# One step for an expert's 32 small list matmuls, and the last expert's row fetch moved ahead of expert 6's first way back, in a fused attention and mixture-of-experts kernel

## The chip, the cores and the metric

The kernel runs on one core of a Trainium2 chip. The metric is the device time in microseconds of one execution of the program; lower is better. Profile times count from the start of the profiled execution's span. The engines are named as the profile does: PE (matmuls), PEld (its weight loads, which overlap), DVE (vector), ACT (activations), POOL (GpSimd, which here also issues all indirect DMAs) and SP (issues the plain DMAs).

## The reference

Four blocks follow each other, each as x = x + layernorm(block(layernorm(x))) over 4096 tokens of width 256: a gated attention, a low-rank feed-forward, a 16-head attention with relu weights, and a mixture of 8 experts. Only the last is touched:

```
S = sigmoid(xt @ Wg).T                    # 8 x 4096 scores
G, I = top_k(S, 1024)                     # each expert picks its 1024 best tokens
ex = xt[I]
hid = gelu(einsum('ekh,ehf->ekf', ex, W1) + b1)
out = (einsum('ekf,efh->ekh', hid, W2) + b2) * G
new_x = zeros_like(xt).at[I].add(out)     # a token may be picked by several experts
```

## The kernel before, in words

The first three blocks end at about 981 us of the span; the experts take the rest. Their stage begins at line 1706. PE, DVE and ACT (and POOL from expert 6 on) run in the order in which the program is written there.

**Search and list.** For each expert a `Search` (line 1757) finds the score of its 1024th token by ten rounds of comparing and counting. A `List` (line 1837) then makes the token numbers: `sort` marks the chosen ones, `rank` counts them (two matmuls and a row of small DVE operations), `chunks` and four `places` build one-hot operands on DVE (line 1914, each 128 x 1024 in bf16), four `collect` multiply them on PE (line 1924, eight 16 x 128 matmuls each, in bf16), ACT copies the result (line 1933), and `gather` folds it with one matmul (line 1936), casts it to `idx` on DVE (line 1938) and issues eight indirect fetches of token rows on POOL (`got`, line 1948). The `places` write tiles `at` from a pool of three buffers, so the fourth can be written only when the first `collect` has read its tile.

**The agenda.** List and search steps are cut into pieces with an assumed DVE cost and the earliest group of tokens beside which they may run (lines 1829 and 1897). `go_on_with_lists(u, time, most)` (line 2300) is called after pieces of expert work; it takes at most one step off the agenda if the time left over from the last is under 0.3, the step is due, and its cost is at most `most`. So the list of expert e+1 is made while expert e runs.

**Expert work.** Experts 0 to 2 and 7 run plain (`feed_forward`, line 2218): 512 tokens a group `u`, two groups an expert. Experts 3 to 6 run both groups at once by seven block products (`feed_forward_by_seven`, line 2168): for each of four f, products a, b, c, d start, then a gets a second product (`a2` below), c a second (`c2`) and d a second (`d2`). Each product shows as two matmuls in the profile. DVE adds between them: u2 + b (line 2194), u2 + c (line 2196, before `c2` may overwrite c), + d (line 2198, before `d2`), and after them lines 2205 and 2208. There are two list calls in each f: one between `a2` and `c2`, with `most` 1.5 (line 2202), and one after `d2` (line 2210).

**The way back.** `project_back` (line 2250) makes four 128 x 256 products `py` for each group; DVE adds the bias and scales by the gate into `y` (lines 2274 and 2275, four buffers), and POOL issues an indirect DMA that adds the rows into `acc_d` in memory (line 2276). Scatters of one expert must wait for those before them, but for expert 6, where they are declared independent.

**The end.** During expert 7 the accumulated rows are read back by SP (`read_back`, line 1996, all six first ones behind every scatter), normalized by DVE statistics, POOL's powers and ACT's scaling (line 2013), and added to the output; expert 7's own rows are fetched by index: `xg`, the block's input rows (`fetch_last`, line 2317, eight fetches), and `accg`, the sums so far (line 2027). The plan `beside_last` (line 2077) says beside which product each of these is put. The final rows go out by indexed scatter (line 2052), behind all other stores. `fetch_last` is called between the two halves of expert 6's way back (line 2214), so its eight POOL fetches stand between that expert's fourth and fifth scatter.

Tile `xs[4]` (`ADDED` is 5) holds input rows of the block; its four stores to `out` are issued before the experts begin, and it is not used after that. `xs[0]` to `xs[3]` already serve as scratch for the seven-product sums (line 2130).

Of the kernel before, what the change touches and what calls it, by code (L numbers as in the profile page):

```python
# [12 lines left out]
BF16 = mybir.dt.bfloat16  # L13
# [6 lines left out]
P = 128  # L20
D = 256
DC = D // P
TB = 512
# [22 lines left out]
NE = 8  # L46
# [5 lines left out]
ADDED = 5  # L52
# [22 lines left out]
def kernel(  # L75
# [33 lines left out]
    B, S, _ = x_in.shape  # L109
# [18 lines left out]
    xs = []  # L128
# [93 lines left out]
    with ExitStack() as st1:  # L222
# [96 lines left out]
        for r in range(2):  # L319
            for j in range(4):  # L320
                at = 32 * j + HD * r
# [126 lines left out]
        wk = st1.enter_context(tc.tile_pool(name="l0", bufs=2))  # L448
# [66 lines left out]
        time = {"now": 0.0, "spent": 0.0}  # L515
# [85 lines left out]
        def open_block(t):  # L601

            d = {"t": t}
            r, stats, _, shift = stats_steps("a", lambda: xs[t])
            d["r"] = r

            def scales(part=slice(0, NJ)):

                if part.start == 0:
                    r["ve"] = small.tile([P, 2, NJ], F32, tag="vea2", name="vea2")  # L610
                    rs = r["both"] = small.tile([P, 2, NJ], F32, tag="rsa2", name="rsa2")
                    r["rs"], r["rs2"] = rs[:, 0, :], rs[:, 1, :]
                ve = r["ve"]
                nc.vector.tensor_scalar(ve[:, 0, part], r["mv"][:, part, 1], EPS, None, ALU.add)
                nc.vector.tensor_scalar(ve[:, 1, part], r["mv"][:, part, 1], 1.0 + EPS, EPS * EPS, ALU.mult, ALU.add)
                nc.gpsimd.tensor_tensor(r["both"][:, :, part], ve[:, :, part], mhalf2[:, :, part], ALU.pow)

            def apply(i0):
                if i0 == 0:
                    d["n"] = wk.tile([P, NJ, D], F32, tag="n", name="n")  # L620
                for i in (i0, i0 + 1):
                    nc.vector.tensor_scalar(
                        d["n"][:, i, :], xs[t][:, i, :], r["mv"][:, i, 0:1], r["rs2"][:, i : i + 1],
                        ALU.subtract, ALU.mult,
                    )

            if t == 0:

                early, late = (lambda part=part: scales(part) for part in halves_0)
                return d, [  # L630
                    *stats[:2], (0.0, early), *stats[2:], (0.0, late), (0.0, lambda: apply(0)), (0.0, lambda: apply(2)),
                    (0.0, shift),
                ]
            return d, [*stats, (0.0, scales), (POW, shift), (0.0, lambda: apply(0)), (0.0, lambda: apply(2))]
# [358 lines left out]
        d, steps = open_block(0)  # L993
# [18 lines left out]
        left, ffn, take = [], ([], [], []), {}  # L1012
        for t in range(NB):
# [51 lines left out]
            left = from_hidden  # L1065
            ffn = feed_forward(t, lambda d=d: d["y"], ahead)
            chains.insert(0, chains.pop())
            d = coming
# [33 lines left out]
    with ExitStack() as st3:  # L1102

        wts = st3.enter_context(tc.tile_pool(name="l1w", bufs=3))
        wk = st3.enter_context(tc.tile_pool(name="l1a", bufs=2))
# [541 lines left out]
        for b in range(B):  # L1647
            after = open_row(None if b else next_hs, last=b + 2 == B) if b + 1 < B else None
            for qh in range(BPB):
# [13 lines left out]
                for q2 in range(halves):  # L1663
                    for g in range(NG):
                        for kt in range(0, KT, halves):
# [5 lines left out]
                            step = kt // halves  # L1671
# [34 lines left out]
    with ExitStack() as st4:  # L1706
# [46 lines left out]
        wk = st4.enter_context(tc.tile_pool(name="moe", bufs=2))  # L1753
        ps = st4.enter_context(tc.tile_pool(name="moe_ps", bufs=2, space=PSUM))
        QT = NTILE // 4

        class Search:
# [71 lines left out]
            def steps(self, behind=0):  # L1829

                spent = 0.15 + 0.6 * len(self.es)
                return [
                    (spent, behind, lambda: self.compare(0)),
                    *((spent + 0.85, behind, lambda r=r: self.tick(r)) for r in range(NBITS // NPER)),
                ]

        class List:


# [57 lines left out]
            def steps(self):  # L1897

                behind = max(QPE * self.e - 3, 0)
                return [  # L1900
                    (0.5, behind, self.sort),
                    (2.6, behind, self.rank),
                    (1.2, behind, self.chunks),
                    (1.4, behind, lambda: (self.places(0), self.places(1))),
                    (1.4, behind, lambda: (self.places(2), self.collect(0), self.places(3), self.collect(1))),
                    (0.3, behind, lambda: (self.collect(2), self.collect(3))),

                    (0.3, behind + 1, self.gather),
                ]

            def places(self, part):
                js = slice(part * QT, (part + 1) * QT)
                self.at[part] = wk.tile([P, P, QT], BF16, tag="at", name="at", bufs=3)
                nc.vector.tensor_tensor(
                    self.at[part],
                    self.lo[:, js].unsqueeze(1).to_broadcast([P, P, QT]),
                    each[:, :, js],
                    ALU.is_equal,
                )
# [37 lines left out]
        lists = [List(e) for e in range(NE)]  # L1957
# [149 lines left out]
        QPE = NC // NJ  # L2107
# [18 lines left out]
        def by_seven(e):  # L2126

            return 3 <= e < NE - 1
# [39 lines left out]
        def feed_forward_by_seven(e):  # L2168

            w1, w2 = weights[e]  # L2170
            hid = [wk.tile([P, FC, TB], F32, tag="hid", name="hid") for _ in range(QPE)]
            (b11, b21), (t3, b22) = ([xT[QPE * e + q][:, c, :] for c in range(DC)] for q in range(QPE))
            t1, t2, t4 = (seven[name] for name in ("T1", "T2", "T4"))
            half = DFF // 2
            s3 = w1[:, 0, half:DFF]
            s1, s2, s4 = (seven[name] for name in ("S1", "S2", "S4"))

            def product(bank, a, b, start, stop, f):
                nc.tensor.matmul(bank, lhsT=a[:, f * P : (f + 1) * P], rhs=b, start=start, stop=stop, skip_group_check=not start)

            gelus = []

            def gelu(n, f, src):
                gelus.append(nc.scalar.activation(hid[n][:, f, :], src, AF.Gelu, bias=mb1[:, e * FC + f : e * FC + f + 1]))

            HC = FC // 2
            for f in range(HC):
                a, b, c, d = (ps.tile([P, TB], F32, tag="mm", name=f"ph{k}", bufs=5) for k in range(4))
                u2 = seven[f"sum{f % 2}"]
                c22, c21, c12 = hid[1][:, HC + f, :], hid[0][:, HC + f, :], hid[1][:, f, :]  # L2190
                product(a, w1[:, 0, 0:half], b11, True, True, f)
                nc.scalar.copy(u2, a)
                product(b, s2, t2, True, True, f)
                nc.vector.tensor_tensor(u2, u2, b, ALU.add)
                product(c, s3, t3, True, True, f)
                nc.vector.tensor_tensor(c22, u2, c, ALU.add)
                product(d, s1, t1, True, True, f)
                nc.vector.tensor_tensor(c22, c22, d, ALU.add)
                product(a, w1[:, 1, 0:half], b21, False, True, f)
                gelu(0, f, a)  # L2200
                if f < HC - 1:
                    go_on_with_lists(QPE * e, 3.2, 1.5)
                gelu(1, HC + f, c22)
                product(c, w1[:, 1, half:DFF], t4, False, True, f)
                nc.vector.tensor_tensor(c21, u2, c, ALU.add)
                gelu(0, HC + f, c21)
                product(d, s4, b22, False, True, f)
                nc.vector.tensor_tensor(c12, u2, d, ALU.add)
                gelu(1, f, c12)
                go_on_with_lists(QPE * e, 3.0)  # L2210
            for q in range(QPE):
                if q == 0 and by_seven(e + 1):
                    weight_sums(e + 1, gelus[-1])
                if q == 1 and e == NE - 2:
                    fetch_last()
                project_back(QPE * e + q, hid[q])

# [74 lines left out]
        searches = [Search(0), Search(1), Search(2, 3), Search(4, 5, 6, 7)]  # L2292
        agenda = []
# [3 lines left out]
                agenda.extend(lists[e].steps())  # L2297
        left = [0.0]

        def go_on_with_lists(u, time, most=4.0):  # L2300
            left[0] = max(left[0] - time, 0.0)
            if agenda and left[0] < 0.3 and agenda[0][1] <= u and agenda[0][0] <= most:
                spent, _, step = agenda.pop(0)
                left[0] += spent
                step()

        first = ps.tile([P, TB], F32, tag="mm", name="idle", bufs=5)
        for n, (_, _, step) in enumerate(searches[0].steps() + lists[0].steps()):
            step()
            if n == 1:  # L2310
                nc.vector.memset(parts[:, 0 : P + NC], 0.0)
            if step == lists[0].rank:
                keep_busy(first, 8)
# [3 lines left out]
        def fetch_last():  # L2317

            for c in range(NC):
                last.fetch(xg[:, c, :], x_d, c)  # L2320

        for u in range(NE * QPE):
            e, q = divmod(u, QPE)
# [44 lines left out]
```

## Time and profile before

| | |
|---|---|
| runs | 1497.52 us median of 3 (1497.13, 1497.52, 1506.65) |
| profiled execution | 1498.18 us, of which the span is 1496.4 us |
| mean granted PE clock | 0.985 |
| busy share of the span | PE 96%, PEld 52%, DVE 63%, ACT 48%, POOL 35% |
| experts, first product of expert 0 to last of expert 7 | 1012.8 to 1484.5 us |
| from PE's last matmul to the end | 11.9 us |
| one DVE `places` operation (line 1914) | 684 ns, 32 of them |
| one indirect fetch of `got` or `xg` on POOL (line 1948) | 1033 ns, and 0.30 us to the next |
| one adding scatter on POOL (line 2276) | 1580 ns, 56 of them |

A timeline row gives the start in us, the duration in us, engine, line, operation, the operands as out<-in with shapes, how many in succession (x16), and in brackets how long the engine had been idle and what ended that. A windows row gives a stretch of the span, its length, the busy time of each engine with the number of instructions, the mean granted PE clock, the DMA share and GB/s.

### The profile page before, as it was taken

How to read it: one execution, taken by the hardware profiler on the slowest of the kernel's cores; microseconds unless marked ns; L12 is line 12 of the kernel's file. 1: busy time of each engine (PE TensorE's matmuls, PEld its weight loads, DVE VectorE, ACT ScalarE, POOL GpSimd, SP SyncE). 2: the span in 40 equal slices, each digit the busy share in tenths (PEclk: the TensorE clock that was granted, in tenths of full speed). 3: DMA queues.
4: the chain of work that ended last, by engine and by line, in shares of the span. 5: the costliest groups of instructions: out<-in, count | busy, mean ns of one | idle time of the engine just before them, and what ended most of it. 6: DMA issues, size and time to landing. Idle time of an engine off the chain costs nothing. (4 is left out here: it accounts for less than half of the span.)

```text
span 1496.4 us, 24269 instructions
## 1 busy us (share of the span) xinstructions
PE 1443.0 (96%) x9240; PEld 780.3 (52%) x9240; DVE 936.5 (63%) x2221; ACT 713.7 (48%) x1182; POOL 518.3 (35%) x646
## 2 busy tenths in 40 slices
PE   8999999999899999999999999949999999999996
PEld 4666666666532333332333235517566656756764
DVE  5456655576456589659974987885545756355355
ACT  4244455444466766777676787722221232232142
POOL 4123231232250223422441323413435324553574
PEclk9999999999999999999999999979999999999998
DMA  8400000002334242533153211151424233343374
GB/s 215 139 1 1 1 1 1 1 0 82 116 99 130 69 135 64 160 99 106 61 183 114 98 52 37 44 162 37 103 29 118 46 87 59 75 100 57 64 189 114
DMA packets 91885, 121.58 MB, mean 81 GB/s; under 512 B 24925, under 2 KB 64250, under 8 KB 91642
## 3 DMA queue, kind: packets, MB, share of 16 engines
q1 hardware_dynamic: 70000, 73.09, 15.6%
q0 software_dynamic: 21712, 46.94, 13.8%
q8 instruction: 72, 1.18, 0.3%
q14 instruction: 43, 0.35, 0.1%
q10 hardware_dynamic: 58, 0.01, 0.0%
HBM read 66.90 MB, written 53.12 MB: 80 GB/s over the span
## 5 line engine op out<-in xcount | busy, mean ns | idle before, releaser
L1542 PE MATMUL po<-w,vaug 128*17 128x512 f32 (+1 forms) x2304 | 269.3, 550 | 2.8 <-DVE turned L1592 2.6
L2259 PE MATMUL py<-w,hid 128*128 128x256 f32 x1024 | 231.0, 383 | 2.1 <-ACT hid L2240 2.1
L2259 PEld LDWEIGHTS py<-w,hid 128*128 128x128 f32 x1024 | 193.3, 192 | 33.1 <-issue 4.7
L1530 DVE TENSOR_SCALAR w<-sc 128x1024 f32<-128x1024 f32 x152 | 184.8, 1221 | 35.2 <-PE sc L1514 32.8
L1522 ACT ACTIVATE w<-sc 128x512 f32<-128x512 f32 x256 | 152.9, 597 | 112.4 <-ACT w L1526 50.5
L1514 PE MATMUL sc<-q,kT 32*128 32x512 f32 (+1 forms) x2304 | 190.5, 412 | 2.2 <-ACT w L1522 1.0
L1514 PEld LDWEIGHTS sc<-q,kT 32*128 32x128 f32 x2304 | 86.2, 183 | 173.7 <-ACT w L1522 92.0
L2276 POOL DMA_INDIRECT acc_d<-y,idx x56 | 88.5, 1580 | 169.3 <-issue 37.4
L2240 ACT ACTIVATE hid<-ph,mb 128x512 f32<-128x512 f32 (+1 forms) x72 | 45.9, 638 | 160.3 <-PE ph L2233 134.5
L1526 ACT ACTIVATE w<-sc 128x512 f32<-128x512 f32 x203 | 120.2, 592 | 0.0
L2233 PE MATMUL ph<-xT,w 128*128 128x512 f32 (+1 forms) x288 | 115.3, 553 | 0.3 <-DVE xT L2124 0.3
L1528 ACT ACTIVATE w<-sc 128x1024 f32<-128x1024 f32 x104 | 106.7, 1026 | 0.0
L1948 POOL DMA_INDIRECT got<-tok_d,idx x64 | 66.1, 1033 | 75.4 <-DVE idx L1938 57.1
L1542 PEld LDWEIGHTS po<-w,vaug 128*17 128x17 f32 x2304 | 41.9, 96 | 95.3 <-issue 71.8
L2233 PEld LDWEIGHTS ph<-xT,w 128*128 128x128 f32 x288 | 52.5, 190 | 51.8 <-issue 47.7
L2274 DVE TENSOR_TENSOR y<-py,mb 128x256 f32<-128x256 f32 x56 | 23.6, 421 | 70.5 <-PE py L2259 55.8
L724 PE MATMUL pg<-nT,wh 128*128 128x512 f32 x128 | 61.6, 613 | 1.5 <-ACT nT L663 1.5
L850 PE MATMUL py<-wo,oT 128*128 128x256 f32 x256 | 61.9, 385 | 0.0
L740 PE MATMUL pv<-wh,nT 128*128 128x512 f32 x128 | 59.7, 593 | 0.0
L850 PEld LDWEIGHTS py<-wo,oT 128*128 128x128 f32 x256 | 47.3, 190 | 17.1 <-issue 9.6
L915 ACT ACTIVATE hid<-ph,vec 128x512 f32<-128x512 f32 x64 | 39.8, 685 | 27.3 <-PE ph L906 27.1
L588 POOL TENSOR_TENSOR x<-x,y 128x1024 f32<-128x1024 f32 x13 | 30.6, 2353 | 57.4 <-ACT y L577 57.4
(340 smaller groups left out, 2399.1 us busy)
## 6 DMA issues: line engine op xcount, KB each, us to landing
q<-q_d POOLq DMA_DIRECT2D x16, 1024.0 KB, 6.0
w<-in_L_ffn_W_dram SPq DMA_DIRECT2D x16, 1024.0 KB
q_d<-parts SPq DMA_DIRECT2D x48, 256.0 KB
kT<-k_d POOLq DMA_DIRECT2D x16, 512.0 KB, 4.1
k_d<-parts SPq DMA_DIRECT2D x24, 256.0 KB
acc_d<-logits SPq DMA_DIRECT2D x8, 512.0 KB
tok_d<-hg SPq DMA_DIRECT2D x30, 128.0 KB
x<-in_L_attn_x_dram SPq DMA_DIRECT2D x7, 512.0 KB
```

The costliest lines, as they stand in the source:

```text
L724: nc.tensor.matmul(pg, lhsT=wh[:, c, HID + e * P : HID + (e + 1) * P], rhs=d["nT"][:, c, :], start=(c == 0), stop=(c == DC - 1),)
L850: nc.tensor.matmul(py, lhsT=d["oT"][:, e, :], rhs=wo[:, e, :], start=(e == 0), stop=(e == EC - 1))
L1514: nc.tensor.matmul(sc[:, m * n : (m + 1) * n], lhsT=row["kT"][t][rows, r, (kt + m) * P : (kt + m + 1) * P], rhs=row["q"][qh, t][rows, r, p ...
L1522: nc.scalar.activation(w[:, 0, :], singles[0], AF.Relu)
L1526: nc.scalar.activation(w[:, 1, :], singles[1], AF.Relu)
L1528: nc.scalar.activation(w[:, 2:4, :], pair, AF.Relu)
L1530: nc.vector.tensor_scalar(w[:, 2:4, :], pair, 0.0, None, ALU.max)
L1542: nc.tensor.matmul(po[32 * j : 32 * j + HD + 1, weighed(halves, r)], lhsT=row["v"][:, kt + m, HQ * t + 4 * r + j, :], rhs=w[:, j, m * n : ...
L1948: return nc.gpsimd.indirect_dma_start(out=dst, out_offset=None, in_=rows[:, :], in_offset=self.at_chunk(c), bounds_check=NT - 1, oob_is_er ...
L2233: nc.tensor.matmul(ph, lhsT=w1[:, c, f * P : (f + 1) * P], rhs=xT[u][:, c, h * n : (h + 1) * n], start=(c == 0), stop=(c == DC - 1),)
L2259: nc.tensor.matmul(py, lhsT=hid[:, f, i * P : (i + 1) * P], rhs=w2[:, f, :], start=(f == 0), stop=(f == FC - 1),)
L2276: scatter = nc.gpsimd.indirect_dma_start(out=acc_d[:, :], out_offset=lists[e].at_chunk(k), in_=y, in_offset=None, bounds_check=NT - 1, oob ...
```

## The change

- A list's four `collect` run in one step, behind all four `places`; before, two of them ran in the step of the later `places`, and two in a step of their own. To make this possible, the third and fourth `places` write into the two halves of `xs[4]`, viewed as bf16, and the pool tile `at` has two buffers.
- The list call in the middle of an f of the seven-product form takes steps by their kind (costs 0.5, 1.2 and 1.4: `sort`, `chunks`, `places`), not by an upper bound on their cost. `collect` and `gather`, at 0.3, can no longer be taken there. The other calls have no bound.
- `fetch_last` is called before the first half of expert 6's way back.
- The first list, which is made ahead of the loop, keeps one `collect` behind each `places` by a function of its own.

```diff
+        def in_stored(half):
+            room = xs[ADDED - 1].rearrange("p j d -> p (j d)")[:, half * TB : (half + 1) * TB]
+            return room.bitcast(BF16).rearrange("p (a b) -> p a b", b=QT)
...
-                    (1.4, behind, lambda: (self.places(2), self.collect(0), self.places(3), self.collect(1))),
-                    (0.3, behind, lambda: (self.collect(2), self.collect(3))),
+                    (1.4, behind, lambda: (self.places(2), self.places(3))),
+                    (0.3, behind, lambda: [self.collect(part) for part in range(4)]),
...
-                self.at[part] = wk.tile([P, P, QT], BF16, tag="at", name="at", bufs=3)
+                if part < 2:
+                    self.at[part] = wk.tile([P, P, QT], BF16, tag="at", name="at", bufs=2)
+                else:
+                    self.at[part] = in_stored(part - 2)
...
-                    go_on_with_lists(QPE * e, 3.2, 1.5)
+                    go_on_with_lists(QPE * e, 3.2, True)
...
-                if q == 1 and e == NE - 2:
+                if q == 0 and e == NE - 2:
                     fetch_last()
                 project_back(QPE * e + q, hid[q])
...
-        def go_on_with_lists(u, time, most=4.0):
+        def go_on_with_lists(u, time, within=False):
             left[0] = max(left[0] - time, 0.0)
-            if agenda and left[0] < 0.3 and agenda[0][1] <= u and agenda[0][0] <= most:
+            if agenda and left[0] < 0.3 and agenda[0][1] <= u and not (within and agenda[0][0] not in (0.5, 1.2, 1.4)):
...
+        def first_places():
+            for part in range(4):
+                lists[0].places(part)
+                if part:
+                    lists[0].collect(part - 1)
+            lists[0].collect(3)
+
+        first_list = [lists[0].sort, lists[0].rank, lists[0].chunks, first_places, lists[0].gather]
```

In the built program the order of instructions moves as follows. On PE the 16 + 16 matmuls of lists 1 to 7 become 32 in a row: for lists 1 and 2 behind the product that stood between the two blocks (list 3, where an expert's way back stood between them, the same), for lists 4 to 7 behind `c2` and `d2` of that f. The fold of lists 5 to 7 comes two products later, and `idx` on DVE behind two more adds. On POOL the eight `xg` fetches come directly behind the eight `got` fetches of list 7, ahead of all eight scatters of expert 6. ACT and SP keep their order. The third and fourth `places` lose their wait on PE and gain none.

## The prediction

> **What bounds the kernel now.** I read the busy shares first, then PE's timeline through the experts, then the chain of waits backwards from the end.
>
> ```profile
> PE 1443.0 (96%) x9240; PEld 780.3 (52%) x9240; DVE 936.5 (63%) x2221; ACT 713.7 (48%) x1182; POOL 518.3 (35%) x646
> ```
>
> PE is busy all but 4%, and the change adds or removes no matmul of weight. So it can only win what PE loses at borders between kinds of matmul, in waits, and in the 11.9 us behind PE's last matmul. PE's timeline inside expert 6 shows a border:
>
> ```profile
> 1371.53 1.02 PE L2179 MATMUL ph<-x,x 128*128 128x512 f32 x2
> 1372.38 1.02 PE L2179 MATMUL ph<-xT,w 128*128 128x512 f32 x2
> 1373.34 1.09 PE L1924 MATMUL parts<-at,pair 128*16 128x128 bf16 x16
> 1374.36 1.12 PE L2179 MATMUL ph<-x,w 128*128 128x512 f32 x2
> 1375.33 1.02 PE L2179 MATMUL ph<-xT,x 128*128 128x512 f32 x2
> ```
>
> Starts count, since matmuls overlap. A product (x2) follows the last one after 0.86 us (1371.53 to 1372.38). The collects begin 0.96 behind their product, 0.10 more; the 16 of them take 1.02; the product after them holds PE 0.97, 0.11 more. A block of collects thus costs 1.02 of work and 0.21 of border.
>
> Expert 4 looks different; there DVE is late, PE's and DVE's timelines say:
>
> ```profile
> 1256.33 1.02 PE L2179 MATMUL ph<-xT,w 128*128 128x512 f32 x2
> 1258.54 1.23 PE L1924 MATMUL parts<-at,pair 128*16 128x128 bf16 x16 [1.18 <-DVE at L1914]
> 1260.53 2.08 PE L2179 MATMUL ph<-x,w 128*128 128x512 f32 x2 [0.77 <-DVE hid L2196]
> 1262.40 1.75 PE L2179 MATMUL ph<-xT,x 128*128 128x512 f32 x2
> 1264.08 1.10 PE L1924 MATMUL parts<-at,pair 128*16 128x128 bf16 x16
> ```
> ```profile
> 1257.07 0.42 DVE L2274 TENSOR_TENSOR y<-py,mb 128x256 f32<-128x256 f32 x1 [3.20 <-DMA acc_d<-y,idx]
> 1259.79 0.69 DVE L2196 TENSOR_TENSOR hid<-x,ph 128x512 f32<-128x512 f32 x1
> ```
>
> DVE stands 3.20 us at a `y` buffer that an earlier scatter still reads, so the add that frees `c2` ends at 1260.48. PE idles 1.18 + 0.77, with one block of collects in between, and `c2` and `d2` then run at half speed (1.87 and 1.68 from start to start, not 0.86).
>
> Last, the end of the kernel: POOL's queue, and the wait on ACT that reaches PE.
>
> ```profile
> 1412.50 1.08 POOL L1948 DMA_INDIRECT xg<-x_d,idx  x1 [0.31 <-issue]
> ...
> 1421.82 1.01 POOL L1948 DMA_INDIRECT xg<-x_d,idx  x1 [0.31 <-issue]
> 1423.13 1.62 POOL L2276 DMA_INDIRECT acc_d<-y,idx  x1 [0.30 <-issue]
> ...
> 1428.78 1.54 POOL L2276 DMA_INDIRECT acc_d<-y,idx  x1 [0.30 <-issue]
> 1433.34 1.08 POOL L1948 DMA_INDIRECT accg<-acc_d,idx  x1 [3.02 <-DMA acc_d<-y,idx]
> ```
> ```profile
> 1468.52 1.09 ACT L2013 ACTIVATE back_w<-back_w,msc,rsc 128x256 f32<-128x256 f32 x2 [4.43 <-POOL msc L2007]
> 1471.07 0.67 ACT L2240 ACTIVATE hid<-ph,mb 128x512 f32<-128x512 f32 x1
> ```
> ```profile
> 1470.23 0.70 PE L2259 MATMUL py<-w,hid 128*128 128x256 f32 x2 [1.29 <-ACT hid L2240]
> 1471.79 12.75 PE L2259 MATMUL py<-w,hid 128*128 128x256 f32 x50 [0.85 <-ACT hid L2240]
> ```
>
> Eight fetches (1.31 us each from start to start) stand in front of the last four scatters, whose rows were ready from 1413.8 on; the last goes at 1428.78 though DVE had its rows at 1425.05. The read-back waits for its landing (3.0 us idle on POOL), and 40 us later this same chain stops PE for 1.29 + 0.85 = 2.14 us: two gelus stand in ACT's queue behind the scaling of the block read back last.
>
> **The change part by part.**
>
> *Joined collects, lists 1, 2, 3, 4, 6, 7.* The 32 matmuls stay; one border of 0.21 goes: 6 x 0.21 = 1.26 us won on PE. The first list had all 32 in a row already (2.43 us from 1003.87): nothing.
>
> *Lost cover.* In lists 4 to 7 the first block stood between `a2` and `c2` and gave DVE 1.23 us for line 2196. Now PE arrives at `c2` earlier. In expert 6 it would arrive at 1373.24, and that add runs from 1372.55 for 0.69: over at 1373.24, and with the 0.05 that `c2` needs after it in expert 4 (1260.48 to 1260.53), 0.05 lost; the same in expert 5 (1317.16 against 1317.15). In expert 3 the add ends at 1212.54, 0.6 early: nothing. Together 0.1 lost. `d2` comes 0.86 behind `c2`, the add it needs 0.79 behind the other: no wait.
>
> *List 5, in expert 4.* The `y` wait stays: POOL's scatters there follow each other at 4.5 us, from a start (the list 4 fetches at 1224.51) that moves with PE, and nothing of it is changed. So `c2` again starts at 1260.53. The block that ran inside the wait for nothing now comes behind `d2`: 1.02 lost. The half speed is the open point. The Trainium skill (TensorE: Matmul & The Clock Gate, "The HAM clock gate") says that PE's clock falls to half after an idle window of about 3.4 us, on a free-running grid, and returns after a busy one. The new gap is 3.34 us in one piece (1257.19 to 1260.53), too short to fill a window, so by that rule the clock would hold and 1.01 + 0.72 = 1.7 us of slow `c2` and `d2` be won. But in the rows here only 1.95 us of idle, split by 1.2 us of matmuls, was enough for half speed; a longer gap will hardly do better. I take the row: +1.0; the rule gives -0.7, and both ends go into the range.
>
> *`places` into `xs[4]`.* Same DVE operation, 684 ns. It loses its wait for PE (4.2 us in two lists), which hid behind DVE idle time: `idx` waits for PE anyway. The stores of `xs[4]` were issued by 851.5, the first of these operations is at 1003: no new wait. Nothing.
>
> *Fold two products later in lists 5 to 7.* 0.03 us of PE either way. The `got` fetches of list 7 start at about 1384.5, not 1382.48: DVE now casts `idx` behind two more adds. For lists 5 and 6 POOL is then up to 2 us later, ahead of a 1.5 to 4.4 us wait for a gelu, hidden by that; without it the weight sums would be late by as much.
>
> *The fetches moved.* On POOL: 16 fetches x 1.315 from 1384.5 end at 1405.5. Expert 6's first scatter goes then instead of at 1400.47, the second at 1407.4 (1403.73), the third 1409.3 (1407.18), the fourth 1411.1 (1410.64). Behind them stands DVE's fifth `y`, at 1413.0, which needs the first one's buffer: 1405.5 plus 3.8 to landing is 1409.3, in time by 3.7 us. The later four go with their rows at 1414.1, 1418.5, 1422.4 and 1425.3: the last is 3.5 us earlier. Down the chain: the six read-backs and `accg` fetches start 3.5 earlier, and POOL's first adding store (1446.28) too, as ACT can scale from 1438.7. Its second (1449.01) stands behind a power whose statistics follow an add of expert 7's product, done only at about 1441.3; it goes at 1446.1, 2.9 earlier. The last read-back stands behind that store, so the ACT scaling at 1468.52 comes at about 1465.6 and the last gelu ends at 1468.9, when PE wants it at 1469.1: PE's 2.14 goes. The final scatters (from 1476.90), behind all stores, start 2.9 earlier, and POOL is then full to the last one at 1488.47 (eight scatters, three powers): the end moves with it, 2.9. Bounds: 3.5 (the scatter's own move) and 0 (DVE and DMA hold the chain where it is); I take 2.9, worked out row by row.
>
> **The sum**: -1.26 + 0.1 + 1.0 - 2.9 = -3.1 us. On the profiled execution, 1498.18 with a span of 1496.4, that is 1495.1; on the median of the runs, 1497.52, it is **1494.4**. Each expert's stage bounds itself by PE, so the parts add.
>
> **The rivals.**
>
> *The end does not follow.* Between 1448 and 1466 the timeline of DMA is nearly full; if the read-backs just queue there, or DVE's rows timed by expert 7's products hold the chain, the move gives nothing: -1.26 + 0.1 + 1.0 = -0.2, so 1497.3. For it: of the chain's steps in the middle, several gain under 1 us. Against it: POOL's and SP's steps stand idle behind the last scatter.
>
> *The clock holds in expert 4.* Another -1.7: 1492.7. Against it, the rows above.
>
> *Slower: the lost cover exposes DVE.* In experts 3, 5 and 6 no block of collects stands before `c2` any more. If DVE is late there as it is in expert 4, PE stands 1.23 us longer and falls to half speed for 1.7: 2.9 each, 8.8 for three, and with the -3.1 the kernel ends at 1503.2. It decides from 1.0 us of new loss in each of the three. Against it: those stages show no DVE wait on a scatter, and the add is late by 0.05 at most.
>
> *The steps do not move as said* is excluded: in the built program the 32 stand in a row.
>
> **How the numbers follow.** Forecast 0.60, end does not follow 0.21, clock holds 0.12, exposed DVE 0.07. The parts of the forecast's own case span -1.2 - 0.7 - 3.5 = -5.4 to about -1.5 (a tail of 1.4): 1492.1 to 1496.0. The second case reaches to 1497.3, and the runs shown, but for one, lie within 0.4 of each other; with about 1 us on both ends for that the range is 1491.0 to 1498.8 and leaves out the slower case and stray runs. One per cent is 15 us, about what a measurement of this kernel can tell from no change; no case reaches it, so faster 0.02, within 0.96, slower 0.02.
>
> **What would show it.** PE's timeline: 32 collects in one row, the product behind them 0.97; 30.45 us for expert 4's products growing by about 1, with 1.18 and 0.77 of idle becoming one gap of 3.3 on line 2196. POOL: `xg` fetches directly behind `got`, last scatter within 0.5 of its `y`. End: no wait of PE on ACT's gelu near 1470, final scatters about 3 us earlier. It is wrong if a `y` wait shows in expert 6 or the 2.14 stays.

## The result, and the profile after

| | before | after |
|---|---|---|
| median of 8 runs each | 1500.87 us | 1491.22 us |
| lowest to highest | 1497.13 to 1506.65 | 1490.54 to 1493.94 |
| profiled execution | 1498.18 us, span 1496.4 | 1490.95 us, span 1488.6 |
| expert 0's first product to PE's end | 471.78 us | 463.67 us |
| PE's end to the end of the span | 11.9 us | 11.7 us |

The ratio of the times is 0.9948, interval 0.9927 to 0.997: 0.5% less. 1491.2 lies in the predicted range, 0.2 above its lower end and 3.2 below the predicted 1494.4. The two profiled executions differ by 7.8 us of span, not by the 3.1 of the sum; PE's starts say where:

| stretch | change in us | predicted |
|---|---|---|
| up to expert 0's first product | +0.43 | 0 |
| lists 1, 2, 3, 4, 6, 7 | -0.36, -0.25, -0.33, -0.27, -0.14, +0.19: -1.16 | -1.26 + 0.1 |
| expert 4 (list 5) | -2.57 | +1.0 |
| expert 7 | -4.36 | -2.14 |
| behind PE's end | -0.2 | the rest of -2.9 |

PE's line of the page, after:

```profile
PE 1437.6 (97%) x9240; PEld 778.7 (52%) x9240; DVE 935.6 (63%) x2221; ACT 714.5 (48%) x1182; POOL 517.4 (35%) x646
```

PE's timeline in expert 6, after; it answers to the first timeline of the prediction:

```profile
1370.09 1.13 PE L2187 MATMUL ph<-x,w 128*128 128x512 f32 x2 [0.18 <-DVE hid L2204]
1371.06 1.02 PE L2187 MATMUL ph<-xT,x 128*128 128x512 f32 x2
1372.01 1.12 PE L1932 MATMUL parts<-at,pair 128*16 128x128 bf16 x16
1372.91 1.14 PE L1932 MATMUL parts<-x,pair 128*16 128x128 bf16 x16
1373.98 1.12 PE L2187 MATMUL ph<-xT,w 128*128 128x512 f32 x2
```

The 32 stand in one row (1372.01 to 1373.98, 1.97 for both blocks), with one border. The bracket of 0.18 is the lost cover of this list: `c2` now stands where DVE's add is not yet over. It is in this profile alone; the seven other profiles of the joined form have no such wait in expert 6.

PE's timeline in expert 4, after, and under it DVE's:

```profile
1255.55 1.02 PE L2187 MATMUL ph<-xT,w 128*128 128x512 f32 x2
1257.88 1.12 PE L2187 MATMUL ph<-x,w 128*128 128x512 f32 x2 [1.30 <-DVE hid L2204]
1258.84 1.02 PE L2187 MATMUL ph<-xT,x 128*128 128x512 f32 x2
1259.79 1.12 PE L1932 MATMUL parts<-at,pair 128*16 128x128 bf16 x16
1260.71 1.12 PE L1932 MATMUL parts<-x,pair 128*16 128x128 bf16 x16
```
```profile
1254.42 0.42 DVE L2282 TENSOR_TENSOR y<-py,mb 128x256 f32<-128x256 f32 x1 [1.33 <-DMA acc_d<-y,idx]
...
1257.13 0.69 DVE L2204 TENSOR_TENSOR hid<-x,ph 128x512 f32<-128x512 f32 x1
```

One gap, but of 1.30 us, not 3.3; the `y` wait is 1.33 instead of 3.20; `c2` and `d2` stand 0.96 and 0.95 apart: full speed.

POOL and PE at the end, after:

```profile
1401.18 1.01 POOL L1956 DMA_INDIRECT xg<-x_d,idx  x1 [0.30 <-issue]
1402.50 1.62 POOL L2284 DMA_INDIRECT acc_d<-y,idx  x1 [0.30 <-issue]
...
1422.02 1.55 POOL L2284 DMA_INDIRECT acc_d<-y,idx  x1 [1.31 <-DVE y L2283]
1426.59 1.08 POOL L1956 DMA_INDIRECT accg<-acc_d,idx  x1 [3.02 <-DMA acc_d<-y,idx]
```
```profile
1460.74 2.31 PE L2241 MATMUL ph<-xT,w 128*128 128x512 f32 x5
1462.88 13.98 PE L2267 MATMUL py<-w,hid 128*128 128x256 f32 x64
```

The last scatter goes with its rows, 1.30 behind the start of expert 7 (before: 4.74). The 64 matmuls of the last way back run through in 13.98 us; before they took 18.34 (1466.20 to 1484.54): 2.14 of waiting, and 2.2 that the prediction did not see. PE's clock was granted at half (0.50) from 1472.07 to 1475.48, as the windows row of before says; half of these 3.41 us, an estimate, is 1.7 of the 2.2.

```profile
1472.07:1475.48 3.41, 3.41 (x9) 2.72 (x9) 3.34 (x8) 0.00 (x0) 0.00 (x0) 0.50 0.64 221
```

### The profile page after: what moved, and what is told of

It reads as the page before. It is cut to its first block, busy times and chain, and to the rows that moved or that the text cites. A ratio compares the mean times of both kernels' runs of the same rounds, so it can differ in the third digit from the quotient of the medians.

```text
span 1488.6 us, 24267 instructions
## 1 busy us (share of the span) xinstructions
PE 1437.6 (97%) x9240; PEld 778.7 (52%) x9240; DVE 935.6 (63%) x2221; ACT 714.5 (48%) x1182; POOL 517.4 (35%) x646
## 3 DMA queue, kind: packets, MB, share of 16 engines
q8 instruction: 72, 1.18, 0.3%
## 5 line engine op out<-in xcount | busy, mean ns | idle before, releaser
L588 POOL TENSOR_TENSOR x<-x,y 128x1024 f32<-128x1024 f32 x13 | 30.6, 2357 | 57.4 <-ACT y L577 57.4
```

## The experiments

At first the end's gain was taken for a thing of the program: the fetches alone were to be worth 4.4 us. The first runs did not bear that out. From the change's second run on, the theory is that the borders (1.2 us) and a shorter gap in expert 4 are gained in every execution, and that the earlier last scatter only gives slack to the read-back, which pays when the read-back is late. Rival: the 9.7 us between the first two medians belong to the program.

The runs come in four groups, each on one chip with the kernel before beside the others. The last three are on three different chips; the record does not name that of the first. A quarter of the runs lie below the "lower quarter"; "over 1497" counts the runs above 1497 us. The ratio is an estimate of its own, not the quotient of the two medians.

| group | kernel | runs | median | lower quarter | highest | over 1497 | ratio to before, interval |
|---|---|---|---|---|---|---|---|
| 1 | before / after | 8 / 8 | 1500.87 / 1491.22 | 1497.6 / 1490.9 | 1506.7 / 1493.9 | 8 / 0 | 0.9948, 0.9927 to 0.997 |
| 2 | before | 43 | 1494.17 | 1492.5 | 1502.3 | 10 | |
| 2 | fetch only | 14 | 1494.14 | 1493.4 | 1496.9 | 0 | 0.9998, 0.9986 to 1.0011 |
| 2 | lists only | 14 | 1492.95 | 1491.3 | 1503.4 | 2 | 0.9996, 0.9978 to 1.0014 |
| 2 | gap filled | 22 | 1494.68 | 1493.0 | 1502.2 | 7 | 1.0008, 0.9996 to 1.002 |
| 3 | before | 50 | 1495.43 | 1492.6 | 1503.5 | 14 | |
| 3 | after again | 11 | 1491.10 | 1490.3 | 1494.5 | 0 | 0.9984, 0.9969 to 0.9999 |
| 3 | after, five `y` | 16 | 1489.50 | 1488.9 | 1493.8 | 0 | 0.9964, 0.9952 to 0.9976 |
| 3 | before, five `y` | 22 | 1494.04 | 1492.5 | 1502.1 | 8 | 0.9993, 0.9977 to 1.001 |
| 3 | outs first | 14 | 1494.03 | 1492.5 | 1495.5 | 0 | 0.9989, 0.9976 to 1.0002 |
| 4 | before | 53 | 1498.05 | 1495.1 | 1507.1 | 30 | |
| 4 | both parts (after) | 15 | 1490.83 | 1490.0 | 1494.2 | 0 | 0.9949, 0.9932 to 0.9966 |
| 4 | fetch only, again | 22 | 1493.86 | 1492.2 | 1498.7 | 2 | 0.9969, 0.9955 to 0.9983 |
| 4 | lists only, again | 22 | 1497.86 | 1493.9 | 1504.6 | 12 | 0.9995, 0.9977 to 1.0013 |
| 4 | after, five `y`, again | 7 | 1488.70 | 1488.6 | 1491.9 | 0 | 0.9941, 0.9918 to 0.9963 |

**Fetch only.**

```diff
-                if q == 1 and e == NE - 2:
+                if q == 0 and e == NE - 2:
```

> The kernel before with one edit: the last expert's fetches ahead of the first half of expert 6's way back. If the end follows the last scatter (my theory): the last scatter goes with its rows, about 3.5 us earlier; the wait of PE on ACT's gelu near 1470 (2.14 us) and the half speed behind it (about 2.2 us) go; time -4.4 us against before, up to -5. If the end is held by DVE or the DMA queues: within 1 us of before. If most of the 7.8 us between the two profiles came from the lists: -1 to -2 us.

Measured: no change of the median where -4.4 was expected, 1492.8 of span. The last scatter goes 1.29 behind expert 7's start and nothing waits near 1470. In this one profile expert 6 took 56.71 us instead of 55.08: PE's completions of the first two `py` came 1.3 and 4.3 us behind where their matmuls' records end. The second profile of this kernel, further down, has 55.08 again, so the moved fetches do not bring that stall in every execution; its cause stays open.

**Lists only**: the changed kernel with `fetch_last` at its old place.

> The changed kernel with the fetches put back between the two halves of expert 6's way back: joined collects, kinds of steps and later fold alone. If joined blocks save one border of 0.21 us each in six lists and expert 4 keeps a gap: -1.2 us plus what expert 4 does (+1.0 to -2.6), so -0.2 to -3.8 us against before, with the 2.14 us wait near 1470 still there. If the lists carried the whole change: -6 to -8 us.

Measured: 463.53 us for the experts, as in the whole change, and no wait of PE near 1470, though the last scatter is as late as before (4.73 behind expert 7's start) and the wait was expected to stay. PE's timeline of the last way back shows it in one row:

```profile
1460.71 13.98 PE L2267 MATMUL py<-w,hid 128*128 128x256 f32 x64
```

So the wait is not in the program alone.

**The kernel before once more.**

> The kernel before, profiled once more. If expert 4's gap depends on how fast one scatter lands beside the weight load: the wait of line 2274 in expert 4 comes out anywhere from 1.3 to 3.2 us, and the clock may or may not fall there. If the gap is fixed by the program: again 3.20 us, and half speed again behind it.

Measured: a span of 1491.4 and 466.50 us for the experts, against 471.78 in the first profile of the same kernel. DVE's timeline shows what was other. This is its wait for the block read back last:

```profile
1458.98 1.40 DVE L1989 BATCH_NORM_STATS2 stc<-back_w 128x6 f32<-128x256 f32 x4 [1.18 <-DMA back_w<-acc_d]
```

In the first profile it ended at 1464.14. The wait of PE that the prediction's tail term removes was in one execution and not in the other.

**Gap filled**: ten spare matmuls ahead of the two products that waited, to keep PE busy there.

```diff
+                    if u == QPE * NE - 1 and i == 0 and f >= FC - 2:
+                        if f == FC - 2:
+                            idle = ps.tile([P, TB], F32, tag="mm", name="idle", bufs=5)
+                        keep_busy(idle, 6 if f == FC - 2 else 4)
```

> The kernel before with ten bf16 matmuls of 512 columns into an unused bank, six ahead of the matmul that waits for gelu 6 and four ahead of the one that waits for gelu 7, in expert 7's second group: PE works through the gap instead of idling. If PE's half speed behind the gap is the clock gate's answer to the idle time: the wait (2.14 us) stays as time, but the slow matmuls behind it go, -1.7 to -2.2 us against before. If they are slow for another reason, such as the gelus or data coming late: no change, or up to +0.5 us.

Measured: inconclusive for the clock. There was no wait to fill in this profile; the fill cost 2.16 us of PE.

**The change again, on another chip.**

> The changed kernel once more, on one chip with the kernel before. Theory A (the lists are the real gain: six joined blocks, 1.2 us, and a shorter gap in expert 4; the earlier last scatter only gives slack to the read-back, worth 4.4 us in an execution whose read-back lands late and nothing in the others): 1 to 4 us under the kernel before, ratio 0.9975 to 0.9993, and no wait of PE near 1470 in either. Rival B (the 9.7 us between the first two medians belong to the program): ratio 0.992 to 0.995. Rival C (lists and fetches together take something from each other, a y wait in expert 6): ratio 0.9995 or more.

Measured: 4.3 us between the medians, a little over theory A's 1 to 4, and ratio 0.9984, inside its 0.9975 to 0.9993; the interval leaves out rival B's 0.992 to 0.995. Expert 4 took 57.38 us with a gap of 1.27.

**Five `y` buffers, after and before** (on the changed kernel and on the old one).

```diff
-                y = wk.tile([P, D], F32, tag="y", name="y", bufs=4)
+                y = wk.tile([P, D], F32, tag="y", name="y", bufs=5)
```

> The changed kernel with five y buffers instead of four. If the gap in expert 4 comes from the y that an earlier scatter still reads, the wait there (1.33 us in the first profile after) goes, the gap on the hid add (1.30 us) goes with it, expert 4 takes about 56.0 us like expert 5 instead of 57.4, and the kernel is 1.0 to 1.5 us faster than the changed one beside it (more in executions where PE falls to half speed there). Rival: DVE is late in expert 4 for another reason (its own work, the list's steps), the gap stays at 1 us or more and the time with it.

> The kernel before with five y buffers and nothing else. If the two gaps (0.6 to 1.2 and 0.77 us) around expert 4's first list block come from the y wait, and half speed of c2 and d2 from the gaps, then expert 4 goes from 59.1 to 60.0 us down to about 56.3, 2.8 us or more, ratio about 0.998. With the wait gone the c2 and d2 of that f start 0.86 us apart. Rival: the half speed has another cause and stays, then only about 1.5 us come. Rival: the gap has another cause, nothing comes.

Measured: the `y` wait, the gaps and the half speed go in both. DVE's timeline of after with five `y`, to be held against the one above:

```profile
1253.21 0.42 DVE L2282 TENSOR_TENSOR y<-py,mb 128x256 f32<-128x256 f32 x1
1255.92 0.69 DVE L2204 TENSOR_TENSOR hid<-x,ph 128x512 f32<-128x512 f32 x1
```

No bracket. Expert 4 takes 55.98 us after and 56.11 before (57.4 to 57.6 and 57.6 to 60.0 with four buffers), so the gap came from the `y` wait. Twice the changed kernel with five `y` was the fastest of its group, by 1.6 and 2.1 us of the median under the changed kernel. Each of these alone is within the scatter of the runs (resampling them gives -4.4 to +0.7 and -4.5 to +1.2 us); the 1.4 and 1.5 us that expert 4 is shorter in the profiles agree with them. The kernel before gained nothing that can be measured (0.9993), and its profile shows what hid it:

```profile
1468.08 1.40 DVE L1989 BATCH_NORM_STATS2 stc<-back_w 128x6 f32<-128x256 f32 x4 [9.34 <-DMA back_w<-acc_d]
```
```profile
1474.17 1.22 PE L2259 MATMUL py<-w,hid 128*128 128x256 f32 x2 [5.76 <-ACT hid L2240]
1475.73 10.53 PE L2259 MATMUL py<-w,hid 128*128 128x256 f32 x40 [0.34 <-ACT hid L2240]
```

The same wait at the end as in the first profile, now 5.76 + 0.34, with two half-clock windows behind it: expert 7 took 64.9 us instead of the 56.1 without a wait. So the wait is real, and comes in some executions.

**Outs first**: the final scatters of the first four blocks ahead of the statistics of the next two.

```diff
-            (1, "i", 0): [(chosen_stats, 4), (chosen_less_mean, 4), (chosen_out, 0, 1), (known, 5), (chosen_sum, 4)],
+            (1, "i", 0): [(chosen_out, 0, 1), (chosen_stats, 4), (chosen_less_mean, 4), (known, 5), (chosen_sum, 4)],
             (1, "i", 1): [
-                (chosen_stats, 5), (chosen_less_mean, 5), (chosen_out, 2, 3, 4), (known, 6, 7), (chosen_sum, 5),
+                (chosen_out, 2, 3), (chosen_stats, 5), (chosen_less_mean, 5), (chosen_out, 4), (known, 6, 7), (chosen_sum, 5),
             ],
```

> The changed kernel with the final scatters of blocks 0 to 3 of expert 7 put ahead of the statistics (and so of POOL's power) of blocks 4 and 5. In the profile after, the first two final scatters stood behind a power whose statistics were not there yet. If POOL's queue sets the tail, it is full from about 1 us earlier and the 11.7 us behind PE's last matmul become 10.5 to 11.0. Rival: the last block's own chain (product, sum, statistics, power, scaling, scatter) sets the tail: 11.7 stays. Rival: the statistics that now come later hold the last blocks: 12 or more.

Measured: 12.4 us behind PE's end, not under 11. POOL's timeline of this kernel:

```profile
1470.41 1.38 POOL L2060 DMA_INDIRECT out_dram<-xg,idx  x1 [7.88 <-DVE accg L2052]
...
1478.92 0.60 POOL L2001 TENSOR_TENSOR rsd<-ved,mhalf 128x1 f32<-128x1 f32 x1 [0.43 <-DVE ved L2000]
...
1483.63 1.04 POOL L2060 DMA_INDIRECT out_dram<-xg,idx  x1 [0.80 <-DVE xg L2056]
```

The first scatter went 8.7 ahead of PE's end instead of 7.8, but the powers came later and POOL then waited for the last blocks: the third of the expected cases. An earlier start of POOL's queue did not shorten the tail here.

**Both parts and each alone, on one chip.**

> The changed kernel, beside each of its halves and the kernel before on one chip. Theory: two separate gains. The lists take about 1.2 us at the borders and up to 1.7 us in expert 4 off every execution; the fetches take nothing off an execution without a wait of PE near 1470, but those with it (2.14 us and 5.76 us in two profiles of the old order, with half speed behind) do not occur. So against the kernel before the lowest times fall by about 2 to 3 us, and no run lies over 1497 us. Median 3 to 5 us lower. Rival (the halves only add up as their medians did on the second chip, 1.2 and 0.0 us): 1 to 1.5 us lower, with runs over 1497 us in the same share as before (about a quarter).

> The kernel before with fetch_last moved and nothing else, again. Theory: the upper end of the times goes (no run over 1497 us, where about a quarter of the runs of before lie), the lower quarter stays within 0.5 us, or is up to 1.6 us higher if the late y of the first profile of this kernel (PE waited 1.35 us in expert 6) belongs to the program; the median falls by 0 to 1.5 us. Rival (the fetches are worth the predicted 2.9 us in every execution): median 2.5 to 3.5 us lower, the lowest times too.

> The changed kernel with fetch_last at its old place, again. Theory: the lower quarter falls by 1.2 to 2.9 us, expert 4 takes about 57.5 us with PE at full speed, and the upper end stays: about a quarter of the runs 5 us or more above this kernel's lower quarter, from the last read-back that lands late. Rival (the lists alone carry the whole change): times like those of both halves together, without an upper end.

> The changed kernel with five y buffers, again, to see whether it is the best of all: 1.3 us under the changed kernel at its side, ratio to before 0.996 to 0.997, expert 4 at 56.0 us without an idle gap. Rival (the 1.6 us between the two on the last chip were chance): the same as the changed kernel within 0.5 us.

Measured: fetch only -4.2 us of the median, lists only -0.2, both -7.2, five `y` on top another -2.1 (expected: 1.3). The halves add up to -4.4, not -7.2; the 2.8 between is within the scatter of the runs (resampling them gives -5.8 to +2.4), so whether the two parts help each other is not shown. The ratio of both parts, 0.9949, lies where rival B of the change's second run had it. Both parts and fetch only came out lower than the theory's numbers (3 to 5 and 0 to 1.5 us; fetch only's lower quarter fell by 2.9 where 0.5 was expected), and two runs of fetch only lie over 1497 where none was expected. The reading that fits is that the late read-back is commoner on this chip than the theory had it (30 of 53 runs of before over 1497, against a quarter in the two groups ahead); no profile of a late one was taken on it, so this is not shown. The lowest runs of before and of fetch only are the same here (1488.6 and 1488.7), so the 4.2 us do not come off every execution. The lists alone keep the upper end (12 of 22 over 1497); their own gain is too small for these runs (the intervals of the two groups reach from -3.4 to +2.1 us).

## Why the prediction was right, and where not

**The joined collects and the lost cover were right in kind, and a little too small.** The pair has -1.16 us over six lists, just the -1.26 + 0.1, but by chance: expert 6 is 0.3 us slower in this profile of after than in the other seven of the joined form. Over all profiles, but for this one and the stall of fetch only, the experts in which these six lists are made take together 291.7 to 291.8 us with split lists and 290.2 to 290.3 with joined ones: -1.5. The term had the 32 collects at 2 x 1.02 us; in one row they take 1.97. The exposed-DVE rival did not come: the largest new wait is the 0.18 shown above.

**List 5 was wrong: +1.0 predicted, -2.57 in the pair, and never a loss.** Over all profiles expert 4 took 57.57 to 59.97 us with split lists and 57.4 to 57.6 with joined ones. Two steps failed. *"The `y` wait stays ... So `c2` again starts at 1260.53"*: the wait is 2.46 to 3.20 in the five profiles of split lists with four `y` and 1.30 to 1.53 in the six of joined ones. POOL issues the scatter at the same place (1.50 and 1.52 ahead of expert 4's start in the first pair), but it lands later. The trace's record of the 16 DMA engines says of before: 15 parts are down 2.4 us behind expert 4's start, the last at 4.1; of after: all 16 at 2.2. At that place the split kernels have a transfer that the changed one has 7.5 us later. The windows rows of before and after for the same stretch (1.0 us ahead of expert 4's start) show it:

```profile
1251.90:1252.90 1.00, 1.00 (x6) 0.87 (x5) 0.96 (x4) 0.00 (x0) 1.00 (x1) 1.00 0.09 16
```
```profile
1251.12:1252.12 1.00, 1.00 (x6) 0.87 (x5) 0.96 (x4) 0.00 (x0) 1.00 (x1) 1.00 0.00 0
```

16 GB/s for 1 us is 16 KB, and the page's queue "q8 instruction" moved 72 packets, 1.18 MB, 16 KB each. In all six profiles of split lists it starts about 0.1 us ahead of expert 4, and one part of the scatter lands 0.6 to 1.7 us behind the other 15. In two profiles of the joined form it starts 0.26 and 0.27 ahead, in the other six 6.4 to 8.0 us behind, and in none of the eight is a part over 0.43 late. What fixes its place was not tried; that it holds up the one part is read from these times, not shown by an experiment.

*"A longer gap will hardly do better"*: the clock held in all eight profiles of the joined form, six of them with a gap of 1.27 to 1.50 us, and in two of the five split ones with four `y`. The gap of 3.34 us for which the rule and the row were weighed never came, so neither was put to the test; that the rule's end (-0.7) was nearer is luck. The last section has the windows.

**The tail was right in its chain and mis-sized in its worth.** The steps moved as worked out: last scatter and `accg` fetch each 3.4 us earlier relative to expert 7 (predicted 3.5), no `y` wait in expert 6, no PE wait near 1470. But the term took the 2.14 us of one execution for a cost of every one, overlooked the half clock behind it, and let the final scatters follow the chain with POOL "full to the last one". They follow PE: the tail is 11.9 us with the wait, 11.8 without it in the second profile of before, 11.7 after. (Lists only, again, has 12.6; why is not known.) POOL was not full: its last scatter waits for DVE, and starts 3.9 and 3.8 us behind PE's end. POOL's rows, before and after:

```profile
1488.47 1.04 POOL L2052 DMA_INDIRECT out_dram<-xg,idx  x1 [0.80 <-DVE xg L2048]
```
```profile
1480.68 1.04 POOL L2060 DMA_INDIRECT out_dram<-xg,idx  x1 [0.80 <-DVE xg L2056]
```

When the last read-back has landed, counted from the start of expert 7:

| | landed after, us | PE's wait |
|---|---|---|
| before; before with five `y` | 40.1; 44.6 | 1.29 + 0.85; 5.76 + 0.34 |
| before again, gap filled, lists only twice | 35.5, 35.3, 35.3, 36.2 | none |
| all eight with the fetches moved | 31.8 to 33.7 | none |

The first row puts the point at which PE begins to wait at 40.1 - 1.29 = 38.8, and 44.6 - 38.8 = 5.8 agrees with 5.76. So the old order has 2.6 to 3.5 us of slack in an execution without the wait, and the new one 5.1 to 7.0: the predicted 3 us are there, as slack. They are worth nothing in an execution whose read-back lands in time; in the two profiles where it is late, expert 7 is 4.4 and 8.8 us longer. Of all runs with the old order 62 of 154 of before and 29 of 80 of its variants lie over 1497 us; with the moved fetches 2 of 107. The rival is that the upper end is only windows of half clock, which come and go everywhere in the kernel (last section). It does not account for all of it: of the runs with the same mean granted clock of 0.985, 27 of 60 with the old order lie over 1497 us, the highest at 1502.2, and none of the 16 with moved fetches, the highest at 1496.0. That the upper end is this wait remains an inference from profiles of both kinds and the counts; runs other than the profiled ones carry no timeline.

In the later of the two late profiles, before with five `y`, 15 of the 16 parts of the read-back were down at 1459.7 and the last at 1468.1, while the DMA share was 0.91 to 1.08 from 1448 to 1464. Why one part is held so long in some executions, and why the upper end is commoner in two of the four groups, stays open.

**The sum.** The range held, with 0.2 us to spare, and -3.1 was not met as a number: the pair of profiles has -7.8, the medians of the three groups -9.7, -4.3 and -7.2. In the pair list 5 came out 3.6 us better than predicted and the end 1.6 better, so the two errors add. Of the three ratios (0.9948, 0.9984, 0.9949) only the second's interval holds 0.998, which -3.1 would be. That 1491.2 still fell inside is luck: between the medians the change was worth 6.6 us more than predicted, but the base, 1497.52 as the median of three runs, was 1500.87 as that of eight. Rival 1 (the end does not follow) has the right worth in an execution without the wait, though not the reason, since the read-back does land earlier; rival 2 (the clock holds in expert 4) is true in all profiles of the changed kernel.

## What to carry to other kernels

A wait read from one profile is one draw: before its length goes into a sum, ask how long what it waits for could take, and how much slack the change gives it; a second profile of the same kernel tells more than a finer reading of the first. A transfer moved earlier paid here in the upper end of the times, not in the lowest. And where DVE stands at a buffer that a scatter still reads, another buffer (here a fifth `y`, 1.4 and 1.5 us of expert 4) is simpler than to arrange the work around the wait.

## What the runs showed of the hardware

**Half speed is set on a grid, and no window has to be idle throughout.** The granted clock in the records changes only on a grid of 3.413 us (in before, its falls at 1260.44 and 1472.07 us are 62 steps apart), whose phase differs from execution to execution. Each fence has a window with PE idle for a part and the one behind it. First fetch only (the split form) and lists only, again (joined), in expert 4:

```profile
1257.19:1260.61 3.42, 2.04 (x18) 0.70 (x18) 3.21 (x6) 0.69 (x1) 1.59 (x1) 1.00 0.75 187
1260.61:1264.02 3.41, 3.41 (x16) 0.98 (x18) 2.58 (x5) 1.44 (x2) 1.58 (x1) 0.50 0.01 1
```
```profile
1258.58:1261.99 3.41, 1.93 (x5) 0.60 (x4) 3.20 (x7) 1.19 (x2) 0.90 (x1) 1.00 0.82 216
1261.99:1265.41 3.42, 3.42 (x36) 1.32 (x35) 1.86 (x4) 1.82 (x4) 1.55 (x1) 1.00 0.15 11
```

PE was busy 2.04 us of the first window and 1.93 of the second, but half speed followed only the first, in which 1.23 of the busy time are collects (128*16 tiles). The first list, ahead of expert 0, has 2.4 us of collects in one window; here both parts, then fetch only, again:

```profile
1006.84:1010.26 3.42, 2.76 (x34) 0.83 (x32) 2.49 (x5) 0.16 (x1) 0.00 (x0) 1.00 0.00 0
1010.26:1013.67 3.41, 3.25 (x10) 1.24 (x11) 1.98 (x8) 0.11 (x1) 2.19 (x2) 0.50 0.15 40
```
```profile
1006.61:1010.02 3.41, 2.78 (x34) 0.83 (x32) 2.50 (x5) 0.12 (x1) 0.00 (x0) 1.00 0.00 0
1010.02:1013.43 3.41, 2.43 (x13) 1.04 (x14) 2.24 (x9) 0.14 (x1) 2.17 (x2) 1.00 0.13 38
```

Half speed followed a window with PE busy for 2.76 us, and not one busy for 1.93 without collects: so a collect counts for less than a full-width matmul. It does not count for nothing: without them the last window would have 0.34 us of work and the first of all 0.81, yet the clock held behind the last one. Two windows with full-width matmuls alone lie on both sides of the limit: 1.49 us busy of 3.41 was enough to hold the clock (lists only, from 391.92), 1.28 of 3.42 was not (before, from 1468.65). But half speed also followed a window busy for 1.95 us, all but 0.1 of it in 32*128 tiles (lists only, again, from 418.91), and one busy for 1.86, 1.65 of it in products with the identity (fetch only, again, from 6.51). What each kind of matmul counts is not shown. The Trainium skill (TensorE: Matmul & The Clock Gate, "The HAM clock gate") has the grid, the 3.413 us and the free phase, which these records agree with; its "≥1 idle window" is not the limit here, since half speed came with PE busy for up to 2.76 us of the window.

**Half-clock windows far from the change move every kernel's time.** Between 380 and 440 us of the span one profile has no half-clock window, six have one and seven have three or four; expert 0's first product then starts at 1011.2, 1012.8 to 1013.5, and 1015.6 to 1016.5. This spread of 5 us is as large as what the change is worth. The phase of the grid does not settle it alone: fetch only and before with five `y` have their first half-clock window at the same 7.91 us, and then one and three of these.
